# A convolution, state-space, attention and expert kernel: Silu by Tanh on ScalarE, with the multiplications on VectorE one stage later

## The chip, the cores and the metric

The kernel runs on one core of a Trainium2 chip. The core has a matrix engine (TensorE, PE in the profile; its loads of weights are PEld), a vector engine (VectorE, DVE), a scalar engine for activation functions (ScalarE, ACT), a fourth compute engine (GpSimd, POOL) and an engine that here only starts transfers (SyncE, SP). Each engine works through its own instructions in their order and waits on semaphores for the others. The metric is the device time of one execution in microseconds (us); the time before is the median of four runs.

## The reference

The input is x of 4 images with 128 channels and 64 x 64 pixels, in float32. Layer 0 normalises x, runs a depthwise 3 x 3 convolution with a Gelu and a matrix, and then a state-space block ("mamba") over the 4096 pixels of an image in four groups of 32 channels. Layer 1 is attention with four heads over the 4096 pixels, followed by eight experts of which two are chosen for each pixel. The part that the change touches is the input of the state-space block:

```
xz = u @ in_proj_w.T
xin, z = jnp.split(xz, 2, axis=-1)
xin = conv_general_dilated(pad(xin), conv1d_w, ...)      # 4 taps along the pixels
xin = jax.nn.silu(xin + conv1d_b[None, :, None])
x_dbl = xin @ x_proj_w.T
dt, Bm, Cm = jnp.split(x_dbl, [R, R + N], axis=-1)
delta = jax.nn.softplus(dt @ dt_proj_w.T + dt_proj_b)
dA = jnp.exp(delta[..., None] * A)
dBu = delta[..., None] * Bm[:, :, None, :] * xin[..., None]
h = dA_t * h + dBu_t ;  y = einsum("bdn,bn->bd", h, C_t) # scan over the pixels
out = y * jax.nn.silu(z) @ out_proj_w.T                  # y with D_skip * xin added
```

Silu(v) is v times the logistic function of v, which is the same as v/2 + v/2 tanh(v/2).

## The kernel before

The pixels of an image are cut into 8 blocks of 512, so there are 32 blocks for the four images. A block's state-space work is split into two halves (p = 0 and 1) of 128 partitions, and a half has 16 states (n). One block, half and state is a unit; there are 1024 units.

The main loop (line 1207) goes through slots, one unit in each. In a slot the engines get, in this order: a read of `rows` (two rows of the state-space matrices, broadcast to all partitions) for the unit three slots ahead, on SP's queue; the copy of the last state on ACT; the decay `da`, an Exp on ACT, for the unit two slots ahead; one group of attention (four matrix products of scores `sc` on PE and two large Exps `pT` on ACT); the unit's scan on DVE (a product into `h`, a scan over `h`, a product into `hc`); and then, between them, pieces of all other work. An earlier unit's `hc` is summed on PE into `y` (after the first half of the first image POOL adds the `hc` of two units first); the weighted sums `av` of the attention group of the slot before close the PE work.

The other work consists of tasks that are written as generators, in two lanes, X and Y. A lane runs one task at a time, and each `yield` ends one of its pieces. A slot advances each lane by two pieces, in the order X second half, Y first half, [sums of `y`], Y second half, [weighted sums], X first half (lines 1234 to 1251). Every instruction goes through a helper that fixes its place on its engine (lines 428 to 449), so nearly all rows of the profile carry line 445, and the order on each engine is the order in which the Python code emits. Lane Y runs the norms and the convolution of a block (`first_norm`, `conv`) and the input stage of each half (`inputs`, line 679); lane X runs what follows a block (`closed`, line 769: keys, queries and values for attention) and the end of attention with the experts (`finished`, line 1000).

The input stage computes `ps` (two matrix products with `inxc`) and `pz` (one with `inz`) in its first piece; both Silus, into `xin` and `zs`, in its second; the products with `wbc` and `wdt` from `xin` in its third; and in its fourth the copy `bc`, which is sent to memory as `bcd`, and the softplus as Abs, Exp, Ln and Relu (`e`, `ln`, `delta`). One slot later five POOL instructions finish `delta` and `du`. The units of this half can then read `rows` from `bcd`, form `da` from `delta`, and scan with `du`. If a unit's input is not ready when the loop wants to fetch its rows, `until` (line 1149) advances the lanes alone.

PSUM for this work is one bank for each lane (`work("X")` and `work("Y")`); the input stage takes the bank of lane X for `pz` and for the product with `wbc`. The set `held` keeps the lanes out of each other's way: `inputs` and `closed` wait while it isn't empty.

ACT computes its functions from tables. Between a Silu and the next Exp stands a load of another table, and so it is between Exp and Ln, and between Exp and Gelu.

Of the kernel before, what the change touches and what calls it, by code (L numbers as in the profile page):

```python
# [12 lines left out]
AF = mybir.ActivationFunctionType  # L13
ALU = mybir.AluOpType
# [22 lines left out]
def conv_mamba_attn_moe_kernel(ctx: ExitStack, tc: tile.TileContext, t: dict):  # L37
    nc = tc.nc
# [34 lines left out]
    inz, cb, dtb, dsk, wbc = (load(k) for k in ("inz", "cb", "dtb", "dsk", "wbc"))  # L73
# [16 lines left out]
    inxc = const.tile([P, 2, P], F32, name="inxc")  # L90
    for j in range(4):
        r = slice(DI * (j % 2), DI * (j % 2) + DI)
        nc.vector.tensor_mul(inxc[r, j // 2, :], inx[r, :], cw[r, j, :])

    amat = const.tile([P, NST], F32, name="amat")
    nc.scalar.activation(amat, alog, AF.Exp)
# [342 lines left out]
    class Queue:  # L439
# [7 lines left out]
    tensor, vector, scalar, gpsimd, sync = (  # L447
        Queue(e) for e in (nc.tensor, nc.vector, nc.scalar, nc.gpsimd, nc.sync)
    )
# [40 lines left out]
    def tmp(lane, name, shape=None):  # L490
        return side.tile(shape or [P, BLK], F32, tag=f"tmp{lane}", name=name, bufs=4)
# [38 lines left out]
    held = set()  # L530
# [148 lines left out]
    def inputs(b, i, p):  # L679

        xn, pairs = xn_of[b, i], pairs_of[b, i]
        r = slice(DI * p, DI * p + DI)
        while held:
            yield
            yield
        held.add("in")
        ps = work("Y")
        summed(ps, [(inxc[:, j, :], pairs[:, p, 2 * j : 2 * j + BLK]) for j in range(2)])
        pz = work("X")
        mm(pz, inz[r, :], xn[r, 3 : 3 + BLK])  # L690
        yield
        xin = mix.tile([P, BLK], F32, name="xin", bufs=2)
        scalar.activation(xin, ps, AF.Silu, bias=cb)
        zs = mix.tile([P, BLK], F32, name="zs", bufs=4)
        scalar.activation(zs, pz, AF.Silu)
        yield

        pb = work("X")
        mm(pb[0:DI, :], wbc, xin)
        ps = work("Y")  # L700
        mm(ps, wdt, xin)
        yield
        held.clear()
        bc = tmp("Y", "bc")[0:DI, :]
        scalar.copy(bc, pb[0:DI, :])
        bcd = dram.tile([2, NST, 2 * BLK], F32, name="bcd", bufs=4)
        send(bcd.rearrange("c n (k q) -> (c n k) q", k=2), bc)

        e = tmp("Y", "e")
        scalar.activation(e, ps, AF.Abs, bias=dtb)  # L710
        scalar.activation(e, e, AF.Exp, scale=-1.0)
        ln = tmp("Y", "ln")
        scalar.activation(ln, e, AF.Ln, bias=1.0)
        delta = mix.tile([P, BLK], F32, name="delta", bufs=2)
        scalar.activation(delta, ps, AF.Relu, bias=dtb)
        yield
        yield

        du = mix.tile([P, BLK], F32, name="du", bufs=2)
        lost = du  # L720
        gpsimd.tensor_scalar(lost, e, 1.0, -1.0, ALU.add, ALU.add)
        gpsimd.tensor_sub(lost, e, lost)
        gpsimd.tensor_add(ln, ln, lost)
        gpsimd.tensor_add(delta, delta, ln)
        gpsimd.tensor_mul(du, delta, xin)
        in_of[b, i, p] = xin, zs, delta, du, bcd
        done.add(("in", b, i, p))
        yield
# [40 lines left out]
    def closed(b, i):  # L769

        if i == 0:
            kqv[b] = [], [], [], dram.tile([P, NTILE * C], F32, name="td")
        kd, qd, vd, td = kqv[b]
        j, u = divmod(i, 2)
        if u == 0:
            kd.append(dram.tile([P, 2, 2 * BLK], F32, name=f"kd{j}"))
            qd.append(dram.tile([P, 2, 2, 2 * BLK], F32, name=f"qd{j}"))
            vd.append(dram.tile([NH, 2, P, NT * 2 * DH], F32, name=f"vd{j}"))
        kd, qd, vd, sj = kd[j], qd[j], vd[j], slice(u * BLK, (u + 1) * BLK)
        s = slice(i * BLK, (i + 1) * BLK)  # L780
        cm = tmp("X", "cm")
        vector.scalar_tensor_tensor(
            cm.rearrange(IMAGE, w=IMG), xn_of[b, i][:, 3:].rearrange(IMAGE, w=IMG), skip,
            y0_rows(b, i), ALU.mult, ALU.add,
        )
        xr = load_x(t["xtok"][b], i, "xr")
        yield
        yield
        ps = work("X")
        for p in range(2):  # L790
            r = slice(DI * p, DI * p + DI)
            mm(ps[r, :], wout[:, p, r], gated.pop((b, i, p)))
        done.add(("freed", b, i))
        yield
        vector.tensor_add(cm, ps, cm)
        gpsimd.tensor_add(by_tile(xr), by_tile(xr), projb[:, None, :].to_broadcast([P, NT, C]))
        yield
        while held:
            yield
            yield  # L800
        held.add("closed")
        ps = transposed("X", by_tile(cm))
        yield
        xt = yield from normalised("X", by_tile(ps))
        held.clear()
        ps = transposed("X", xt)
        yield
        f = tmp("X", "f")
        scalar.activation(f, ps, AF.Identity, bias=lnb, scale=lnw)
        yield  # L810
        ps = work("X", [P, NT, C])
        for j in range(NT):
            mm(ps[:, j, :], f[:, j * P : (j + 1) * P], projT)
        yield
        tt = side.tile([P, NT, C], F32, name="tt")
        vector.tensor_add(tt, ps, by_tile(xr))
        send(tsave[b][:, s], tt.rearrange("p j c -> p (j c)"), 2)
        xt = yield from normalised("X", tt)

        tr = tmp("X", "tr", [P, NT, C])  # L820
        gpsimd.tensor_add(tr, tt, crow[:, None, :].to_broadcast([P, NT, C]))
        send(td[:, s], tr.rearrange("p j c -> p (j c)"), 2)
        ps = transposed("X", xt)
        yield
        xa = tmp("X", "xa")
        scalar.copy(xa, ps)
        yield
        for d, w, bias in ((kd, wkn, bkn), (qd, wqn, bqn)):
            ps = work("X")
            mm(ps, w, xa)  # L830
            yield
            hi = side.tile([P, BLK], F32R, name="hi", bufs=2)
            vector.tensor_scalar(hi, ps, bias, None, ALU.add)
            lo = side.tile([P, BLK], F32R, name="lo", bufs=2)
            vector.scalar_tensor_tensor(
                lo, ps, bias, hi.bitcast(F32), ALU.add, ALU.subtract
            )
            for half, w in enumerate((hi, lo)):
                w = w.bitcast(F32)
                if len(d.shape) == 4:  # L840
                    send(d[:, :, half, sj], w[:, None, :].to_broadcast([P, 2, BLK]))
                else:
                    send(d[:, half, sj], w)
            yield
        ps = work("X", [P, NT, NH, DH])
        for j in range(NT):
            mm(ps[:, j].rearrange("p h d -> p (h d)"), xa[:, j * P : (j + 1) * P], wv)
        yield
        vector.tensor_copy(vst[:, :, :, 0:DH], ps.rearrange("p j h d -> p h j d"))
        send(vd[:, u].rearrange("h p q -> p h q"), vst.rearrange("p h j d -> p h (j d)"))  # L850
        yield
# [275 lines left out]
    def advance(lane, second):  # L1127

        if inside[lane] != second:
            return False  # L1130
        while True:
            if lane not in running:

                tasks = lanes[lane] if lanes[lane] or slot < len(units) else lanes["X"]
                if not tasks or not all(k in done for k in tasks[0][2]):
                    return False
                key, stages, _ = tasks.popleft()
                running[lane] = key, stages(lane) if callable(stages) else stages
            key, stages = running[lane]
            try:  # L1140
                next(stages)
                inside[lane] = not second
                return True
            except StopIteration:
                assert not second
                done.add(key)
                del running[lane]

    def until(key):
        while key not in done:  # L1150
            flush()
            count = len(done)
            moved = [
                advance(*half) for half in (("X", True), ("Y", False), ("Y", True), ("X", False))
            ]
            assert any(moved) or len(done) > count, key

    blocks = [(b, i) for b in range(B) for i in range(NB)]
# [5 lines left out]
    X, Y = lanes["X"], lanes["Y"]  # L1164
# [42 lines left out]
    while slot < len(units) or due or waiting or left or later or lanes["X"] or running:  # L1207
# [13 lines left out]
        if slot < len(units):  # L1221
# [3 lines left out]
            b, i, p, n = unit  # L1225
# [10 lines left out]
        while due and due[0][0] <= slot:  # L1236
            _, unit, term, first = due.popleft()
            b, i, p, n = unit
# [9 lines left out]
        if waiting:  # L1248
            weighted(waiting)
        waiting = group  # L1250
        advance("X", False)
        while later and later[0][0] <= slot:
            next(later.popleft()[1])
        slot += 1
# [6 lines left out]
    with tc.If(nc.values_load(general[0:1, 0:1]) > 0):  # L1261
# [4 lines left out]
        with tc.For_i(0, B, 1) as b:  # L1266
# [6 lines left out]
            with tc.tile_pool(name="ps_again", bufs=4, space=PSUM) as psum:  # L1273
                for i in range(NB):
                    ps = anew(t_tok[:, NT * i : NT * (i + 1), :], psum)
# [92 lines left out]
```

## Time and profile before

| | |
|---|---|
| median of four runs | 5598.81 us (5596.36 to 5607.02) |
| profiled execution, time | 5593.6 us |
| its span, first to last instruction | 5591.3 us |
| mean granted TensorE clock | 0.945 |
| instructions | 60586 |
| table loads on ACT | 319 in the main part, 409.3 us |
| DVE scan instructions | 1024, 1492 us |
| ACT `pT` | 2048, 1983.7 us |

The page gives the busy time of each engine, the same over 40 equal slices of the span, and groups of equal instructions. A group's row names the line, the engine, the operation, what is written and what is read, the shapes and the count; behind the first bar stand the busy time and the mean duration of one in ns; behind the second the time that the engine was idle just before them, and what ended it. A timeline row has the start, the duration, the instruction and, in brackets, the idle time before it with its releaser. In a view by windows each row is a stretch of time with the busy time of each engine, the granted clock of PE, the share of the transfer engines and GB/s. The chain that ended last covers only the last 12 us here and is not used.

The span falls into a start without attention (to about 390 us), a stretch up to 670 us where attention has begun and pauses, the long middle, and from 4957 us on an end in which the scans are done and attention and the experts finish.

### The profile page before, as it was taken

The page shows a single profiled execution, that of the slowest core. Times are in us where ns is not written, and L with a number is a line of the kernel's source. Part 1 is how long each engine was busy: PE and PEld are TensorE (multiplying, and loading weights), DVE is VectorE, ACT ScalarE, POOL GpSimd, SP SyncE. Part 2 cuts the span into 40 slices and gives each one's busy share as a digit, 9 for nine tenths or more (in the row PEclk, how much of TensorE's full clock was granted, in tenths as well). Part 3 has the DMA queues.
Part 4 walks back from the last instruction along what each step waited for, and adds up shares of the span by engine and source line. Part 5 has one row for each costly group of instructions (what it writes and reads, how often), then busy time and mean ns, then how long its engine had stood idle before and what let it go on. Part 6 is the DMA issues. An engine that isn't in the chain of part 4 may idle for free. (4 is left out here: it accounts for less than half of the span.)

```text
span 5591.3 us, 60586 instructions
## 1 busy us (share of the span) xinstructions
PE 4909.8 (88%) x17866; PEld 2038.1 (36%) x17866; DVE 4177.6 (75%) x6275; ACT 3892.6 (70%) x5957; POOL 2160.5 (39%) x1885
## 2 busy tenths in 40 slices
PE   4666798998999898999998899898999999899997
PEld 2222233333333333333333333333333333344443
DVE  4888877887888888888887888887888888741221
ACT  3455587777777777788777777687777777766553
POOL 2333444454444444445443444345444443320000
PEclk7777799999999999999999999999999999999998
DMA  2455565666666666666665556666666666654432
GB/s 94 168 172 175 193 208 209 208 220 216 230 207 202 216 211 214 209 223 232 224 213 192 196 199 210 219 220 213 230 224 207 204 202 209 211 183 154 148 121 67
DMA packets 427635, 1097.91 MB, mean 196 GB/s; under 512 B 48401, under 2 KB 131746, under 8 KB 427298
## 3 DMA queue, kind: packets, MB, share of 16 engines
q1 hardware_dynamic: 426130, 1093.17, 58.0%
q8 instruction: 144, 2.36, 0.2%
q14 instruction: 193, 1.58, 0.1%
q10 hardware_dynamic: 1168, 0.80, 0.0%
HBM read 941.95 MB, written 135.00 MB: 193 GB/s over the span
## 5 line engine op out<-in xcount | busy, mean ns | idle before, releaser
L445 ACT ACTIVATE pT<-sc 128x1024 f32<-128x1024 f32 x2048 | 1983.7, 1022 | 1011.1 <-PE sc L445 1008.6
L445 PE MATMUL av<-pT,v 128*64 128x512 f32 x8192 | 2001.4, 609 | 3.5 <-ACT avs L445 3.4
L445 DVE TENSOR_TENSOR_SCAN h<-da,state,h 128x512 f32<-128x512 f32 x896 | 1310.3, 1462 | 114.7 <-ACT da L445 22.8
L445 PE MATMUL sc<-qs,ks 128*128 128x512 f32 x4096 | 1304.0, 439 | 98.3 <-DMA ks<-kd 53.6
L445 POOL TENSOR_TENSOR hc<-hc 128x512 f32<-128x512 f32 x448 | 654.8, 1462 | 1722.8 <-DVE hc L445 1516.4
L445 PEld LDWEIGHTS sc<-qs,ks 128*128 128x128 f32 x4096 | 715.8, 193 | 771.2 <-ACT pT L445 282.1
L445 PEld LDWEIGHTS av<-pT,v 128*64 128x64 f32 x8192 | 501.7, 137 | 1194.5 <-issue 1104.0
L445 DVE TENSOR_TENSOR h<-rows,du 128x512 f32<-128x512 f32 x1024 | 834.2, 815 | 87.2 <-ACT state L445 36.9
L445 DVE TENSOR_TENSOR hc<-rows,h 128x512 f32<-128x512 f32 x1024 | 804.1, 785 | 78.2 <-DVE h L445 2.3
L445 ACT ACTIVATE da<-delta,amat 128x512 f32<-128x512 f32 x1024 | 749.4, 732 | 9.5 <-DVE h L445 5.2
L445 PE MATMUL y<-hc,ident 128*128 128x512 f32 x1152 | 665.8, 666 | 62.1 <-DVE hc L445 51.3
L445 ACT ACT_TABLE_LOAD x319 | 409.3, 1283 | 23.2 <-PE ps_Y L445 18.0
L445 ACT COPY state<-h 128x1 f32<-128x1 f32 x896 | 175.6, 196 | 194.6 <-DVE h L445 193.9
L445 PEld LDWEIGHTS y<-hc,ident 128*128 128x128 f32 x1152 | 219.9, 210 | 213.9 <-DVE hc L445 101.7
L445 POOL TENSOR_SCALAR rsY<-mvY 128x4 f32<-128x4 f32 x99 | 57.1, 576 | 523.3 <-DVE mvY L445 519.3
L445 POOL TENSOR_TENSOR avs<-avs,prev 128x512 f32<-128x512 f32 x64 | 91.8, 1434 | 430.3 <-ACT avs L445 306.1
L445 PE MATMUL ps_X<-share,w_ew 128*128 128x512 f32 x448 | 225.4, 626 | 20.5 <-DVE share L445 19.8
L445 ACT ACTIVATE xt<-ps_Y,shiftY,rsY 128x128 f32<-128x128 f32 x380 | 143.3, 462 | 133.0 <-POOL shiftY L445 125.5
L445 POOL TENSOR_SCALAR du<-e 128x512 f32<-128x512 f32 x64 | 146.0, 2282 | 215.2 <-ACT e L445 215.2
L445 DVE TENSOR_TENSOR share<-share,xf 128x1024 f32<-128x1024 f32 x128 | 181.9, 1421 | 52.0 <-DMA share<-sharesY 30.3
L445 DVE RECIPROCAL den<-den 128x32 f32<-128x32 f32 x16 | 5.5, 347 | 265.4 <-DMA den<-total 265.3
L445 DVE TENSOR_TENSOR_SCAN h<-da,h 128x512 f32<-128x512 f32 x128 | 181.7, 1419 | 15.5 <-ACT da L445 2.5
(234 smaller groups left out, 4722.3 us busy)
## 6 DMA issues: line engine op xcount, KB each, us to landing
rows<-bcd SPq DMA_DIRECT2D x1024, 512.0 KB
ks<-kd SPq DMA_DIRECT2D x256, 512.0 KB
qs<-qd SPq DMA_DIRECT2D x129, 512.0 KB
v<-vd SPq DMA_DIRECT2D x256, 256.0 KB
share<-sharesX SPq DMA_DIRECT2D x112, 512.0 KB
pairs<-xn SPq DMA_DIRECT2D x128, 128.5 KB
qd<-hi SPq DMA_DIRECT2D x32, 512.0 KB
qd<-lo SPq DMA_DIRECT2D x32, 512.0 KB
```

Source lines behind the costliest of these rows:

```text
L445: return lambda *args, **kw: queued(op(*args, **kw))
```

## The change

The weights `inxc`, `inz` and the bias `cb` are halved once at the start, so that `ps` with its bias and `pz` hold v/2. ACT computes Tanh of both. Two half slots later DVE computes, with scalar_tensor_tensor, xin = (ps + cb) * t, then xin = (ps + cb) + xin, and zs = (zs + 1) * pz. The stage's later pieces move back by one slot. Since `pz` now stays in lane X's bank for a slot longer, a new member "z" of `held` stops lane X's first half from advancing until DVE has read it. The sets are emptied by name instead of as a whole.

```
+    for w in (inxc.rearrange("p j c -> p (j c)"), inz, cb):
+        nc.vector.tensor_scalar_mul(w, w, 0.5)
...
-        held.add("in")
+        held.update(("in", "z"))
...
         xin = mix.tile([P, BLK], F32, name="xin", bufs=2)
-        scalar.activation(xin, ps, AF.Silu, bias=cb)
+        t = tmp("Y", "t")
+        scalar.activation(t, ps, AF.Tanh, bias=cb)
         zs = mix.tile([P, BLK], F32, name="zs", bufs=4)
-        scalar.activation(zs, pz, AF.Silu)
+        scalar.activation(zs, pz, AF.Tanh)
+        yield
+        yield
+        vector.scalar_tensor_tensor(xin, ps, cb, t, ALU.add, ALU.mult)
+        vector.scalar_tensor_tensor(xin, ps, cb, xin, ALU.add, ALU.add)
+        vector.scalar_tensor_tensor(zs, zs, 1.0, pz, ALU.add, ALU.mult)
+        held.discard("z")
         yield
...
-        held.clear()
+        held.discard("in")
...
-        held.clear()
+        held.discard("closed")
...
-            moved = [
-                advance(*half) for half in (("X", True), ("Y", False), ("Y", True), ("X", False))
-            ]
+            moved = [advance("X", True), advance("Y", False), advance("Y", True)]
+            moved.append("z" not in held and advance("X", False))
...
-        advance("X", False)
+
+        if "z" not in held:
+            advance("X", False)
```

## The prediction

> **What bounds the kernel now.** I read the busy time of the engines first, then the stretches, then the neighbourhood of the instructions that change. The page (engine, busy us, share; then busy tenths in 40 slices of 140 us):
>
> ```profile
> PE 4909.8 (88%) x17866; PEld 2038.1 (36%) x17866; DVE 4177.6 (75%) x6275; ACT 3892.6 (70%) x5957; POOL 2160.5 (39%) x1885
> ...
> PE   4666798998999898999998899898999999899997
> ...
> DVE  4888877887888888888887888887888888741221
> ACT  3455587777777777788777777687777777766553
> ```
>
> TensorE (PE) leads in all but the first five slices; there VectorE (DVE) does. Three stretches (us of each engine in the order PE, PEld, DVE, ACT, POOL, then the granted clock):
>
> ```profile
> 390.00:670.00 280.00, 189.36 (x456) 76.68 (x458) 238.48 (x335) 146.13 (x275) 108.73 (x96) 0.76 0.53 180
> 670.00:4860.00 4190.00, 3809.93 (x14232) 1581.38 (x14230) 3457.38 (x5043) 3171.47 (x4877) 1857.23 (x1569) 0.97 0.63 213
> 4960.00:5420.00 460.00, 447.87 (x1810) 189.14 (x1810) 91.14 (x250) 270.50 (x322) 38.30 (x51) 0.99 0.44 143
> ```
>
> From 670 to 4860 us PE is busy 91%, DVE 83%, ScalarE (ACT) 76%. Ten of the 64 input stages lie before 670 us; I look at the 52 that follow (Silu at 679 to 4674 us) and leave the last two out. The rows that the change touches (count, busy us, mean ns), and two of the operation that it adds:
>
> ```profile
> L445 ACT ACT_TABLE_LOAD x319 | 409.3, 1283 | 23.2 <-PE ps_Y L445 18.0
> ...
> L445 ACT ACTIVATE xin<-ps_Y,w_cb 128x512 f32<-128x512 f32 x64 | 44.0, 688 | 31.6 <-PE ps_Y L445 30.9
> ...
> L445 ACT ACTIVATE zs<-ps_X 128x512 f32<-128x512 f32 x64 | 37.8, 591 | 6.8 <-PE ps_X L445 6.5
> ...
> L445 DVE SCALAR_TENSOR_TENSOR lo<-ps_X,w_bkn,hi 128x512 fp32r<-128x512 f32 x32 | 24.0, 751 | 1.1
> ...
> L445 DVE SCALAR_TENSOR_TENSOR cm<-ps_Y,w_fc2b,y 128x512 f32<-128x512 f32 x32 | 23.8, 742 | 13.8 <-PE ps_Y L445 13.8
> ```
>
> I cut the trace at the start of the Silu of each of the 52 stages and summed 5 us windows: 0 to 5, 5 to 10 and 10 to 15 us after it.
>
> ```profile
> sum 260.00, PE 245.88 PEld 89.76 DVE 186.38 ACT 232.82 POOL 80.96; mean PE 4.73 PEld 1.73 DVE 3.58 ACT 4.48 POOL 1.56
> sum 260.00, PE 255.05 PEld 92.95 DVE 154.22 ACT 236.03 POOL 89.50; mean PE 4.90 PEld 1.79 DVE 2.97 ACT 4.54 POOL 1.72
> sum 260.00, PE 200.47 PEld 75.98 DVE 186.03 ACT 256.70 POOL 239.78; mean PE 3.86 PEld 1.46 DVE 3.58 ACT 4.94 POOL 4.61
> ```
>
> ACT is full (90, 91, 99%), DVE has 4.9 us of 15 free, and PE idles, but mostly in the third window (23%). Whether the table loads cause that idling is the whole question. A typical stage:
>
> ```profile
> 2382.84 1.28 ACT L445 ACT_TABLE_LOAD   x1
> 2384.13 0.69 ACT L445 ACTIVATE xin<-ps_Y,w_cb 128x512 f32<-128x512 f32 x1
> 2384.72 0.59 ACT L445 ACTIVATE zs<-ps_X 128x512 f32<-128x512 f32 x1
> 2385.32 1.28 ACT L445 ACT_TABLE_LOAD   x1
> 2386.62 0.72 ACT L445 ACTIVATE da<-delta,amat 128x512 f32<-128x512 f32 x1
> 2387.69 1.94 ACT L445 ACTIVATE pT<-sc 128x1024 f32<-128x1024 f32 x2 [0.35 <-PE sc L445]
> ...
> 2390.16 0.69 ACT L445 ACTIVATE e<-ps_Y,w_dtb 128x512 f32<-128x512 f32 x1
> ```
>
> ```profile
> 2389.00 1.12 PE L445 MATMUL ps_Y<-xin,wdt 128*128 128x512 f32 x2
> 2397.03 0.73 PE L445 MATMUL sc<-qs,ks 128*128 128x512 f32 x2 [1.18 <-ACT pT L445]
> ```
>
> The two loads around the Silus are absorbed: by `pT` ACT waits for PE again, and `e` starts 0.04 us after the matmul `wdt` ends (2390.12). PE's idle 1.18 us comes from what follows: `e`, Exp, load, Ln, Relu, load, `da`, `pT`, 6.87 us against 5.73 us of PE work. The change leaves that chain as it is. Of the 52 stages 35 show less than 0.11 us from the end of `wdt` to `e`; in the other 17 it is 0.47 to 2.28 us, 17.6 us in all.
>
> **The change part by part, in us.**
>
> *Removed.* Tanh needs no load next to Exp: the built program has 193 table loads, before 320. 127 x 1.283 = 163 off ACT. On the path is only what delays `e`: at least 0, at most both loads in each of the 52 stages, 52 x 2.57 = 134. I take the 17.6 measured, and 7 for the clock: after 7 of those 17 stages the granted clock is 0.5 for 27 in all, half of which is lost, and I give half of that back. -25. *The trace and a rule:* In the rows above `da` starts 0.02 after the load before it has ended. The Trainium skill (ScalarE: Activation LUTs, What ACT_TABLE_LOAD costs) adds a drain of about 1380 ns to every load, 2.66 us a switch; by it 338 would leave ACT, and the upper bound would be 277. No drain shows here, so the sum goes by 1.283.
>
> *Tanh for Silu.* Same shapes and operands, priced like the Silu rows (688 and 591 ns): 0. The loads also waited for PE's matmul; Tanh waits for it itself.
>
> *Added on DVE.* 192 scalar_tensor_tensor at 0.745 (the rows lie at 742 and 751): 143, 2.24 a stage. They stand a slot after the Tanhs, behind that slot's scan. What hides them in the 52 stages is DVE's lead. I measured it as the time from the end of a slot's `hc` to PE's first score two slots on: median 8.7; in the slots from one before the input stage to two after it at least 9.0, median 10 to 14; from three to eight slots after it at least 4.2 (stages from slot 200 on). In before DVE reaches that place between 4.3 before and 4.3 after the Silu's start, about when both Tanhs would end (1.28 of load less, 1.28 of two Tanhs), so that what it may wait there fits into the lead too. Cost 0; without the lead 52 x 2.24 = 116. Behind them in DVE's queue stands the next slot's `h`, for which ACT's copy of the state and PE's sum `y` wait, both after the lead. In the ten stages before 670, where DVE is the bound (85% from 390 to 670), it is 0 to 10 x 2.24 = 22; in the 15 us after the Silu DVE is idle 3.0 a stage there (last 8 of the ten), which hides a part. I take +10.
>
> *Moved.* `wbc`, `wdt`, `bc`, `e` to `du` and the send of `bcd` come one slot later, and following both slot loops I find that the stage of half p = 0 also begins one slot later (the longer stage of p = 1 stands before it in lane Y): two slots in all, three at the first block of an image. What is late next is `da` of that half, which stands in ACT's queue ahead of `pT`. From the end of POOL's `delta` to that `da` before shows 5.2 to 48, median 14. The two slots ahead of that `da` last 7.4 in the median. Of the 27 blocks after 670 us two fall short when 8.1 goes off, 3.7 in all, and thirteen when 14.6 does (three slots of 4.86), 44 in all. I take +5. SP's read of `rows` still comes a slot or more after the send of `bcd`. Lane X loses one slot a stage; it is idle in 299 of 1024 scan slots before and in 247 after: 0.
>
> *Order of attention.* Before, attention finds its keys unready in slots 465 to 469; on resuming PE waits 5.9 for `ks`, and two stretches of 6.8 at half clock (6.8 lost) lie there. In the changed loop those empty slots don't occur (1200 slots instead of 1204, attention starting one later). Bounds 0 and -13; I take -12, since the work itself only moves.
>
> *Setup.* Three small multiplies, and two DVE steps (1.5) in the first chain against one load saved (1.28): 0.
>
> Sum: -25 + 10 + 5 - 12 = -22. The profiled execution took 5593.6 (span 5591.3), 5.2 under the median of 5598.81; so 5571.6 for it and 5577 for a median.
>
> **Rivals.**
> 1. *All loads count* (gain 134 instead of 25). For it: ACT at 90% and more for 15 us, DVE idle beside it. Against: PE at 95 and 98% in the first 10 us, `e` on time in 35 of 52. 5598.8 - 134 - 12 + 15 = 5468; with half of it, 5535.
> 2. *No change.* PE bounds these stages, and what ACT gains is waited away at the same `pT`; the empty slots come back elsewhere. For it: the same idle 1.18 us after the Ln chain. Against: the 17 late stages. 5599.
> 3. *Slower: `delta` is late.* With input stages 14.6 later ACT stands at `da`, `pT` behind it and PE behind that: 44, and after each of the 13 waits half clock for 3.4, 13 x 1.7 = 22; with DVE's part before 670 in full (22) and the 25 + 12 gained kept: +51, 5650. With a shift of 12.5 ten blocks fall short by 20 in all: 20 + 17 + 22 - 37 = +22, 5621. It decides from a shift of about 10 (2 short blocks at 9.7, 10 at 12.5). Against: ACT waited for `delta` once so far, 2.3 us.
> That the loads stay is ruled out by the program.
>
> **How the numbers follow.** Forecast 0.48, rival 1 0.12, rival 2 0.17, rival 3 0.23. The predicted time is the forecast's, 5577; its own range is 5560 to 5592. The range to hold 8 in 10 reaches past half of rival 1 and the lower form of rival 3: 5525 to 5625. Within 0.2% is 5587.6 to 5610.0, about what a measurement can tell from no change; an edge of the forecast (0.03) lies in it. Faster 0.45 + 0.12 = 0.57, same 0.20, slower 0.23.
>
> **What would show it.** 193 loads and some 247 us in their row; ACT 160 less busy, DVE some 140 more; `e` within 0.1 us of `wdt` in nearly all stages; PE's idle of about 1.2 us before `sc` still there; DVE's lead never under 2 us; no large wait of ACT `da` for POOL `delta`. Wrong is the forecast if PE's idle time from 670 to 4860 us (380 us now) falls by much more than 30 us, if ACT waits for `delta` in more than a few blocks, or if PE waits for `xin` behind DVE.

## The result, and the profile after

The changed kernel takes 5603.64 us (median of 39 runs, 5589.63 to 5622.63); the kernel before, measured beside it, 5596.43 us (60 runs). The ratio is 1.0014, with a 95% interval of 1.0009 to 1.0019: slower by 7.8 us, where 22 us less were forecast. The profiled execution has a span of 5601.4 us (5591.3 before) at a mean granted clock of 0.946 (0.945).

The busy times on the page of the changed kernel, with PE, DVE and ACT in the 40 slices (here 140 us each):

```profile
PE 4903.2 (88%) x17866; PEld 2057.2 (37%) x17866; DVE 4332.8 (77%) x6470; ACT 3735.2 (67%) x5830; POOL 2166.8 (39%) x1885
...
PE   4666698998899899998999899898989899999997
...
DVE  4889887888888888888898888888888888851221
ACT  2444577777777677677677667677667777766553
```

ACT has lost 157 us of work and DVE has gained 155. PE's busy time fell by 6.6, but the span grew by 10.1. The same two stretches as before:

```profile
390.00:670.00 280.00, 179.59 (x433) 73.17 (x431) 243.95 (x342) 130.95 (x260) 104.66 (x90) 0.79 0.53 181
670.00:4860.00 4190.00, 3810.04 (x14254) 1602.34 (x14256) 3588.42 (x5188) 3040.12 (x4768) 1857.19 (x1568) 0.97 0.63 213
```

In the long middle PE is busy 3810.0 us, as before (3809.9): what ACT gave up there did not let PE run more. In the stretch up to 670 us DVE is busier by 5.5 us and PE by 9.8 less. The changed rows of the page's groups, ACT first:

```profile
L448 ACT ACTIVATE pT<-sc 128x1024 f32<-128x1024 f32 x2048 | 1983.9, 1022 | 1117.2 <-PE sc L448 1114.4
...
L448 ACT ACT_TABLE_LOAD x192 | 246.3, 1283 | 3.4
...
L448 ACT ACTIVATE t<-ps_Y,w_cb 128x512 f32<-128x512 f32 x64 | 43.9, 686 | 56.3 <-PE ps_Y L448 55.9
L448 ACT ACTIVATE zs<-ps_X 128x512 f32<-128x512 f32 x64 | 38.1, 596 | 25.8 <-PE ps_X L448 25.8
```

```profile
L448 DVE SCALAR_TENSOR_TENSOR xin<-ps_Y,w_cb,xin 128x512 f32<-128x512 f32 x64 | 48.1, 751 | 2.3
L448 DVE SCALAR_TENSOR_TENSOR xin<-ps_Y,w_cb,t 128x512 f32<-128x512 f32 x64 | 47.8, 747 | 39.6 <-ACT t L448 39.4
...
L448 DVE SCALAR_TENSOR_TENSOR zs<-zs,ps_X 128x512 f32<-128x512 f32 x64 | 43.4, 678 | 1.1 <-ACT zs L448 1.1
```

192 loads are left of 319, and the new operations cost what the rows before had promised: 139 us on DVE, 82 on ACT. The first row says where the 163 us of loads went. Before, it read:

```profile
L445 ACT ACTIVATE pT<-sc 128x1024 f32<-128x1024 f32 x2048 | 1983.7, 1022 | 1011.1 <-PE sc L445 1008.6
```

ACT's idle time ahead of `pT`, always until PE delivers `sc`, rose by 106 us: two thirds of the freed time is now waiting for PE. A stage of the changed kernel, ACT alone:

```profile
2407.67 0.69 ACT L448 ACTIVATE t<-ps_Y,w_cb 128x512 f32<-128x512 f32 x1 [0.18 <-PE ps_Y L448]
2408.73 0.60 ACT L448 ACTIVATE zs<-ps_X 128x512 f32<-128x512 f32 x1 [0.37 <-PE ps_X L448]
2409.22 0.71 ACT L448 ACTIVATE da<-delta,amat 128x512 f32<-128x512 f32 x1
2412.37 1.94 ACT L448 ACTIVATE pT<-sc 128x1024 f32<-128x1024 f32 x2 [2.44 <-PE sc L448]
...
2420.83 1.28 ACT L448 ACT_TABLE_LOAD   x1
```

No load stands around the Tanhs any more, and ACT waits 2.44 us for PE behind them and one `da`.

How far the two executions are at the same unit shows where the difference arises. The columns are the starts of four scans and the end of the last `pT`, in us; a slot is counted by the unit that is scanned in it, 256 to an image:

| | slot 150 | 256 | 512 | 1023 | last `pT` |
|---|---|---|---|---|---|
| before | 673.6 | 1145.1 | 2413.6 | 4956.3 | 5516.1 |
| after | 678.5 | 1153.6 | 2436.7 | 4981.1 | 5527.5 |

8.5 us are lost in the first image (up to slot 256), 14.6 from there to 512, next to nothing (1.7) from 512 to the last scan, and 13.4 come back in the tail. The tail and the middle belong together: attention has no empty slots at 465 to 469 any more, so that 252 `pT` lie between slots 384 and 512 instead of 240, and 303 instead of 312 are left for the tail.

### The profile page after: what moved, and what is told of

The parts are those of the page before. It is cut to its first block, busy times and chain, and to the rows that moved or that the text cites. A ratio compares the mean times of both kernels' runs of the same rounds, so it can differ in the third digit from the quotient of the medians.

```text
span 5601.4 us, 60582 instructions
## 1 busy us (share of the span) xinstructions
PE 4903.2 (88%) x17866; PEld 2057.2 (37%) x17866; DVE 4332.8 (77%) x6470; ACT 3735.2 (67%) x5830; POOL 2166.8 (39%) x1885
## 4 chain that ended last, share of the span: by engine, by line
PE 46%; DVE 24%; ACT 11%; issue 7%; POOL 6%; DMA 5%; SPq 1%; DVEq 0%; ACTq 0%; POOLq 0%
PE av L448 17%; DVE h L448 12%; PE sc L448 10%; PE ps_X L448 9%; PE ps_Y L448 5%; PE y L448 4%; ACT pT L448 3%; ACT xt L448 2%; DVE hc L448 2%; DVE cm L448 2%; ACT L448 2%; POOL rsX L448 2%; POOL rsY L448 1%; DMA inv<-inverse 1%; ACT e L448 1%
## 5 line engine op out<-in xcount | busy, mean ns | idle before, releaser
L448 PE MATMUL sc<-qs,ks 128*128 128x512 f32 x4096 | 1312.2, 441 | 65.1 <-ACT pT L448 35.5
L448 DVE TENSOR_TENSOR_SCAN h<-da,state,h 128x512 f32<-128x512 f32 x896 | 1291.8, 1442 | 97.1 <-ACT da L448 6.5
L448 DVE TENSOR_TENSOR h<-rows,du 128x512 f32<-128x512 f32 x1024 | 867.2, 847 | 38.5 <-DMA rows<-bcd 14.9
L448 PE MATMUL y<-hc,ident 128*128 128x512 f32 x1152 | 644.7, 646 | 61.1 <-DVE hc L448 55.5
L448 POOL TENSOR_SCALAR rsY<-mvY 128x4 f32<-128x4 f32 x99 | 56.8, 573 | 658.4 <-DVE mvY L448 656.1
L448 PE MATMUL ps_X<-ident,xt 128*128 128x128 f32 x372 | 95.5, 329 | 120.3 <-ACT xt L448 113.2
```

What stands on the lines that cost most here:

```text
L448: return lambda *args, **kw: queued(op(*args, **kw))
```

## The experiments

All ratios are to the kernel before, measured beside it on the same chip; in brackets is the 95% interval. Behind a ratio, us are the ratio less 1, times 5596. Each run has one profile, of one execution; its span can lie some us off the run's median. Two suspects stood at the start: the new order (a longer stage, lane X held) and DVE's added work; open was whether the table loads had been worth anything.

**New order alone.** The changed kernel, but ACT computes Silu as before, without halved weights and without the multiplications.

```
-        t = tmp("Y", "t")
-        scalar.activation(t, ps, AF.Tanh, bias=cb)
+        scalar.activation(xin, ps, AF.Silu, bias=cb)
...
-        scalar.activation(zs, pz, AF.Tanh)
+        scalar.activation(zs, pz, AF.Silu)
...
-        vector.scalar_tensor_tensor(xin, ps, cb, t, ALU.add, ALU.mult)
-        vector.scalar_tensor_tensor(xin, ps, cb, xin, ALU.add, ALU.add)
-        vector.scalar_tensor_tensor(zs, zs, 1.0, pz, ALU.add, ALU.mult)
```

> The new order alone: the input stage is one slot longer and lane X is held back with z as in the changed kernel, but ACT computes Silu as before (320 table loads) and DVE gets no multiplications. Theory A (the loads were worth the 25 us predicted, and the longer stage with lane X held costs about 36): ratio to before 1.004 (+24 us = 36 - 12 for the empty attention slots). Theory B (loads worth nothing, the multiplications on DVE cost what was lost): 0.998 (-12 us). Theory C (loads worth nothing, the order costs about 10): 1.000, and lane X's waits (PE ps_X for DVE prX, for ACT xt and xf) as long as in the changed kernel.

Measured 1.0003 [0.9994, 1.0012], +1.7 us. The size is theory C's, but the next run speaks against its other half, that the loads are worth nothing. The scan of slot 150 starts at 658.4, 15 us earlier than before: the longer stage helps the first image (it does so alone too, further down). And though all 319 loads are there, `e` starts within 0.04 us of the end of `wdt` in every stage from 670 us on but the last. What cured the late `e` is the new order, not the missing loads.

**Loads back.** The changed kernel with a Silu of one column ahead of the Tanhs.

```
+        scalar.activation(spare, spare, AF.Silu)
         scalar.activation(t, ps, AF.Tanh, bias=cb)
```

> The changed kernel with a Silu of one column ahead of the two Tanhs in each input stage, so that the two table loads per stage are back (about 320 loads, 1.28 us each, 163 us of ACT), and the rest as in the changed kernel. Theory A: +18 to +25 us on the changed kernel, ratio to before 1.005 to 1.006, and e comes late again in some stages. Theory B and C: within 6 us of the changed kernel, ratio 1.001 to 1.0025. If all loads count: +134 us, ratio 1.025.

Measured 1.0045 [1.0031, 1.0059], 17 us above the changed kernel, a little under theory A. But no `e` is late here either, again but for the last. The page of this run:

```profile
PE 4913.0 (87%) x17866; PEld 2055.0 (37%) x17866; DVE 4328.0 (77%) x6470; ACT 3904.9 (70%) x6021; POOL 2169.6 (39%) x1886
```

Its span is 5616.5, 15.1 above the changed kernel's, and 9.8 of that is PE's busy time for the same 17866 matmuls. Stretches at half clock between 670 and 4860 us sum to 242 us here and to 222 in the changed kernel. Each of the 55 stretches here follows 3.4 us in which PE was busy 61% or less (91% is the mean from 670 to 4860 us). So in these two profiles the loads cost less by waiting than by the lower clock that PE is granted after waiting. A second pair further down, Silu in the first image without and with the loads behind it, agrees: 14.8 of the 24.0 us between its spans are PE's busy time. How much of this is the chance of single executions is open: the kernel before, with all its loads, has the same 242 us.

**DVE's work twice.** The changed kernel with three more multiplications a stage.

```
+        junk = side.tile([P, BLK], F32, name="junk")
+        vector.scalar_tensor_tensor(junk, ps, cb, t, ALU.add, ALU.mult)
+        vector.scalar_tensor_tensor(junk, ps, cb, t, ALU.add, ALU.add)
+        vector.scalar_tensor_tensor(junk, t, 1.0, pz, ALU.add, ALU.mult)
```

> The changed kernel with three more multiplications of the same shapes on DVE in each input stage, into a tile that nobody reads (192 more, 2.24 us a stage, 143 us of DVE). Theory A and C (DVE's work is hidden by its lead behind 670 us and costs only in the first image, 8.5 us measured for the first three): +8 to +12 us on the changed kernel, ratio to before 1.003. Theory B (DVE's work is what costs): +20 us or more, ratio from 1.005 up, to 1.024 if none of it is hidden.

Measured 1.0134 [1.0118, 1.0151], 67 us above the changed kernel for 140 us of DVE. This is far from hidden: in the two profiles 20 us arise before slot 150, 28 before 256, 46 before 512. Not all of it is the price of DVE's time: the new multiplications also read the lanes' two banks, and PE waits 14.9 us for `junk` itself before it can write lane X's.

**Lane X not held.** ACT copies `pz` out of lane X's bank.

```
-        held.update(("in", "z"))
+        held.add("in")
...
+        zc = mix.tile([P, BLK], F32, name="zc", bufs=1)
+        scalar.copy(zc, pz)
...
-        vector.scalar_tensor_tensor(zs, zs, 1.0, pz, ALU.add, ALU.mult)
-        held.discard("z")
+        vector.scalar_tensor_tensor(zs, zs, 1.0, zc, ALU.add, ALU.mult)
```

> The changed kernel in which ACT copies pz out of lane X's bank right behind its Tanh (64 copies more, about 0.6 us each by the zs row, 38 us of ACT) and DVE multiplies from the copy, so that z is no longer held and lane X loses no slot. Theory A (holding lane X is what costs): ratio to before 0.995 to 0.999, the waits of PE ps_X for DVE prX back to about 25 us. Theory B: no gain, 1.001 to 1.004. Theory C: 0.999 to 1.000 if it is the hold, 1.001 or more if it is the longer stage.

Measured 1.0042 [1.0028, 1.0056], 16 us above the changed kernel. Freeing lane X did not help; with 37 us of copies on ACT in the same run it is not shown what the hold alone costs. PE's waits for `prX` fell from 47.0 only to 36.9.

**Silu in the first image.** (`cbf` is a copy of the bias, made before the halving.)

```
+        if b == 0:
+            scalar.activation(xin, ps, AF.Silu, bias=cbf, scale=2.0)
+            scalar.activation(zs, pz, AF.Silu, scale=2.0)
+        else:
+            scalar.activation(t, ps, AF.Tanh, bias=cb)
+            scalar.activation(zs, pz, AF.Tanh)
...
+        if b > 0:
             vector.scalar_tensor_tensor(xin, ps, cb, t, ALU.add, ALU.mult)
...
```

> The changed kernel, but for the first image (16 of the 64 input stages, all before slot 256) ACT computes Silu of twice the halved input, so that DVE gets no multiplications there; the other three images and the order of all work are as in the changed kernel. If the multiplications cost their time only where DVE is the bound, in the first image (19 to 24 us by the two looks that differ in them alone), and the loads there cost nothing: 19 to 24 us below the changed kernel, ratio to before 0.997 to 0.998, faster than both. If the multiplications cost evenly over the stages (16 of 64): about 6 us below the changed kernel, ratio 1.000. If the loads are worth as much in the first image as elsewhere: 4 us less gain than the first.

Measured 0.9997 [0.9986, 1.0008]: 9.5 us below the changed kernel, level with before. In its profile slot 150 is reached 15 us earlier (663.5), slot 256 also 15. The ratio gives less than the 19 to 24 expected for a price paid in the first image alone, and its uncertainty of some 7 us reaches to the 6 us of a price spread evenly over the stages.

**Longer stage alone.** The kernel before with two empty pieces.

```
         scalar.activation(zs, pz, AF.Silu)
+        yield
+        yield
```

> The kernel before with its input stage one slot longer (two empty pieces behind the Silus), without the hold on lane X, and nothing else changed (320 loads, no multiplications on DVE). If it is the longer stage that lets the first image end 15 us earlier and brings attention past its empty slots: scan of slot 150 at about 658 us as with the new order alone, ratio to before 0.999 to 1.001. If the hold on lane X cost something on top: up to 10 us below the new order alone, ratio 0.9985. If delta came late by the shift: over 1.003, with waits of ACT da for POOL delta beyond 10 us.

Measured 0.9992 [0.9981, 1.0002], -4.5 us, the low end. Slot 150 starts at 650.7, 23 us earlier than before. Most of it is given back: the stretch from slot 150 to 256 takes 6 more, the tail 10 more (318 `pT` left instead of 312). Of the 54 stages behind 670 us 8 still have an `e` more than 0.11 us behind `wdt`, 8.9 us in all (19 and 20.2 us before, the last two stages with them): the longer stage alone cures only a part.

**DVE's work alone.** The kernel before with three more multiplications in each stage.

```
         mm(ps, wdt, xin)
         yield
+        junk = side.tile([P, BLK], F32, name="junk")
+        for _ in range(3):
+            vector.scalar_tensor_tensor(junk, xin, cb, xin, ALU.add, ALU.mult)
```

> The kernel before with three scalar_tensor_tensor of 128x512 more on DVE in each input stage, into a tile that nobody reads (xin as input, no PSUM), everything else as before. If the first image pays for them in full and the rest hides them: +19 to +24 us, ratio 1.0034 to 1.0043, nearly all of it before slot 256. By the prediction's value (a third of them hidden in the first image as well, 0 behind it): +10 us, 1.0018. If nothing is hidden: +143 us, 1.026.

Measured 1.0055 [1.0039, 1.0071], +31 us. In the profile 10 of it have arisen by slot 150, 15 by slot 256, and the rest behind the first image, where the prediction had put 0. (These multiplications are dearer than the change's own, 872 ns; see the last section.)

**Stage as short as before.** The changed kernel without the two slot halves.

```
         scalar.activation(zs, pz, AF.Tanh)
         yield
-        yield
         vector.scalar_tensor_tensor(xin, ps, cb, t, ALU.add, ALU.mult)
...
         mm(ps, wdt, xin)
-        yield
         held.discard("in")
```

> The changed kernel with the two slot halves taken out again: the multiplications come one half earlier, and the products with wbc and wdt in the same half as the softplus chain, so that the stage is as long as before; z still holds lane X for a slot. If the longer stage costs something in the changed kernel (delta late, attention moved): 5 to 10 us below it, ratio to before 0.9995 to 1.0005. If the longer stage gains 15 us in the first image, as the new order alone showed: 5 to 15 us above the changed kernel, 1.002 to 1.004. If ACT now waits for the products (e directly behind wdt in its queue): more than that, with a wait of ACT e for PE ps_Y of 1 us a stage or more.

Measured 1.0088 [1.0075, 1.0101], 41 us above the changed kernel. Slot 150 starts at 705.6, 27 us later. ACT's idle time ahead of `e` is 26.7 in all (24.2 in the changed kernel), so the third case is out; the first image loses. The stage's added slot is a gain, and without it the changed kernel is 41 us slower.

**DVE's work behind the first image, in one burst or spread.** The kernel before with 144 multiplications more.

```
+    flat = taps.rearrange("p k c -> p (k c)")[:, 0:BLK]
+    def burn():
+        junk = side.tile([P, BLK], F32, name="junk")
+        for _ in range(3):
+            vector.scalar_tensor_tensor(junk, flat, cb, flat, ALU.add, ALU.mult)
...
         mm(ps, wdt, xin)
         yield
+        if b > 0:
+            burn()
```

The spread kernel has one multiplication in `burn` and calls it in the main loop:

```
         advance("Y", True)
+        if 256 <= slot < 1024 and slot % 16 in (0, 5, 10):
+            burn()
```

> The kernel before with three scalar_tensor_tensor of 128x512 more on DVE in each of the 48 input stages of the last three images (144 in all, into a tile that nobody reads, inputs in SBUF), none in the first image. The prediction's step (DVE's lead hides them): within 4 us of before, ratio 1.000. If they delay the pieces of lane X and Y that PE waits for on DVE: +12 to +20 us, ratio 1.002 to 1.0036, with PE's waits of ps_X for DVE and ACT pieces some 10 us longer and the scan of slot 150 where before has it (674 us).

> The same 144 scalar_tensor_tensor more on DVE in the last three images, but one at a time in every fifth slot or so (slots 0, 5 and 10 of each 16) instead of three in a row in the slot of the input stage. If the sum of DVE's work counts: as the three in a row, +12 to +20 us. If the burst of 2.24 us is what delays lane X and a single 0.75 us fits between: less than half of the three in a row, 0 to +8 us, ratio below 1.0015.

In a burst 1.0036 [1.0023, 1.0049], +20 us; spread 1.0072 [1.0059, 1.0085], +40. The lead doesn't hide this work, and spreading it, which I expected to be cheaper, costs twice as much. That fits the prediction's finding that DVE has more time beside the input stage than elsewhere; but the spread multiplications also stand at another place in the slot, and what of the difference is due to that isn't shown. In the spread run's profile PE idles 403 us from 670 to 4860 us (380 before), and its busy time for all matmuls is 17 us more, with 290 us at half clock there (242 before). The order of all instructions on PE, ACT and POOL is that of the kernel before, so PE's waits from 670 to 4860 us can be set side by side (engine, what waits, for what: us in total, times, longest). Before:

```profile
PE ps_X L445 <- ACT xt L445: 51.2, 43, 4.0
...
PE ps_X L445 <- DVE prX L445: 23.1, 13, 9.0
...
PE ps_X L445 <- DVE share L445: 19.8, 16, 2.4
...
PE ps_X L445 <- DVE aT L445: 12.7, 6, 5.2
```

With the burst:

```profile
PE ps_X L445 <- ACT xt L445: 56.5, 44, 4.0
...
PE ps_X L445 <- DVE prX L445: 30.5, 16, 10.1
PE ps_X L445 <- DVE share L445: 24.9, 21, 2.4
...
PE ps_X L445 <- DVE aT L445: 18.1, 6, 7.0
```

These four, all for products into lane X's bank, grow by 23.2 us; `xt` itself is made by ACT from statistics that come from DVE through POOL. PE's whole idle time in this stretch grows from 380 to 393, since other waits shrink (the one for `ks` from 41.1 to 35.3). The scan, on the other hand, keeps its lead: from the end of `hc` to PE's first score two slots on it is 8.7 us in the median before, 8.6 with the burst, 8.8 in the changed kernel and 8.6 with DVE's work twice.

**Longer stage in the first image only,** by one slot and by two.

```
         scalar.activation(zs, pz, AF.Silu)
+        if b == 0:
+            for _ in range(4):
+                yield
```

(these lines are the second kernel's; the first has two empty pieces)

> The kernel before with its input stage one slot longer in the first image only (two empty pieces behind the Silus where b is 0), nothing else changed. If the longer stage is what let the first image end 15 to 23 us earlier in the two looks that have it: scan of slot 150 at 650 to 660 us, and 12 to 20 us below before, ratio 0.9965 to 0.998, faster than both kernels. If that gain is given back between slots 150 and 512: ratio 0.999 to 1.000.

> The same with two slots more instead of one in the first image. If what helps is only that DVE's queue gets past the wait for the input chain: no further gain, within 5 us of one slot more. If delta and du come late for the next half: 5 us or more slower than one slot more, with waits of DVE h for POOL du and of ACT da for POOL delta before 670 us.

One slot: 0.9998 [0.9987, 1.0008]; slot 150 at 658.1, but the gain is gone by the end. Two slots: 0.9983 [0.9974, 0.9992], 9.5 us below before, and the only kernel here whose interval lies below 1. Its slot 150 starts at 651.5, the last `pT` ends at 5502.6, and from 104 us to the end of the first image neither DVE nor ACT waits for a late `du` or `delta`. Why two slots keep their gain and one doesn't, these runs don't show.

**The loads back behind the first image.** The run with Silu in the first image, plus

```
         else:
+            scalar.activation(spare, spare, AF.Silu)
             scalar.activation(t, ps, AF.Tanh, bias=cb)
```

> The changed kernel with Silu on ACT in the first image (as in the earlier run of that kind), and in the other three images a Silu of one column ahead of the Tanhs, so that all 320 table loads are back. Against the run without these loads it gives the loads' worth behind the first image: 15 to 17 us if they add up (ratio to before 1.0025 to 1.003). Against the new order alone (1.0003) it gives what the multiplications cost behind the first image: +13 us if they add up, 0 if DVE's lead hides them (ratio 1.0003).

Measured 1.0021 [1.0011, 1.0030]. Without these loads it was 0.9997: they are worth 13 us. Against the new order alone (1.0003) the multiplications behind the first image cost 10 us; the two intervals together leave some 7 us either way. Both near what was expected if the terms add.

This pair has the change's own order and its own multiplications, and PE works through the same instructions in the same order in both. From slot 256 to slot 1023 PE idles 340 us with the new order alone and 355 here. With the new order alone, from 670 to 4860 us:

```profile
PE ps_X L446 <- ACT xt L446: 62.5, 43, 3.6
PE ps_X L446 <- DVE prX L446: 48.3, 17, 5.0
...
PE ps_X L446 <- DVE cm L446: 17.5, 14, 2.2
```

With the multiplications behind the first image:

```profile
PE ps_X L450 <- ACT xt L450: 68.5, 43, 3.8
PE ps_X L450 <- DVE prX L450: 48.7, 17, 5.4
...
PE ps_X L450 <- DVE cm L450: 20.8, 18, 2.6
```

Here it is `xt` and `cm` that PE waits for longer; `prX`, `share` (22.6 to 20.7) and `aT` (16.9 to 16.6), which grew with the burst, don't. The wait for `prX`, 23.1 before, has doubled by the new order alone.

**The hold alone.** The kernel before with `z` held from the first piece of the stage to the third.

```
-        held.add("in")
+        held.update(("in", "z"))
...
         scalar.activation(zs, pz, AF.Silu)
         yield
+        held.discard("z")
...
-        advance("X", False)
+        if "z" not in held:
+            advance("X", False)
```

> The kernel before with the hold z on lane X alone: set with the input stage's first piece, released in its third, so that lane X loses one slot a stage; stage length, Silu, loads and DVE's work as before. If lane X's lost slot costs what the difference of two runs says: +6 us, ratio 1.001. If the prediction's 0 holds: 1.000 within 0.0005. If it moves attention as the new order does (no empty slots at 465 to 469): tail after the last scan about 547 us instead of 560.

Measured 1.0005 [0.9995, 1.0015], +3 us with 0 inside the interval: as a price of the hold inconclusive. What it does to attention is plain: 303 `pT` are left after the last scan, in 548 us. So it is the hold, not the longer stage (318 left), that brings attention past its empty slots, and this run is the test of that term: -12 was predicted for it, with 0 for the hold, and the interval from -3 to +8 leaves that out. The hold alone also makes `e` late more often, in 34 of the 54 stages.

**Both.** Silu, no hold and two slots more in the first image, the changed stage in the others.

```
         if b == 0:
             scalar.activation(xin, ps, AF.Silu, bias=cbf, scale=2.0)
             scalar.activation(zs, pz, AF.Silu, scale=2.0)
...
+        if b == 0:
+            held.discard("z")
+            yield
+            yield
```

> First image: Silu on ACT, no hold on lane X, the input stage two slots longer (the run with that alone was at 0.9983). Other images: as in the changed kernel, with Tanh and the multiplications on DVE. If the terms add: 0.9983 plus what the changed stage is worth behind the first image (-17 loads, +13 multiplications, +5 hold, all of it within 5 us of 0): ratio 0.9975 to 0.9990, faster than both kernels. If attention's order eats it: 0.9995 or more.

Measured 0.9995 [0.9985, 1.0006]. This is what was expected if the gain of the longer first image is not kept; the interval still reaches into the range of terms that add. Of the kernels measured the one to use is the one before with two slots more in the first image.

## Why the prediction was wrong

Four runs lie on a path from before to after, each step changing one main thing:

| step | predicted, us | measured, us |
|---|---|---|
| before to the new order alone: `delta` later (+5), empty slots (-12), lane X held (0) | -7 | +1.7 |
| to the multiplications in images 2 to 4 (loads still there) | 0 | +10 |
| to the multiplications in the first image too | +10 | +13 |
| to the kernel without the loads | -25 | -17 |
| sum | -22 | +7.8 |

The second and third steps also hold Tanh for Silu and the small Silus that bring the loads back (203 ns each on ACT); the fourth takes these out again. Each step is a difference of two ratios with some 5 to 10 us of uncertainty; the sum is the measured result. By that the first two steps lie clear of their forecast, by 8.7 us with an uncertainty of 5 and by 10 with 7; the last two don't.

- **The step that failed** is "What hides them in the 52 stages is DVE's lead ... Cost 0". The lead was measured for one product of DVE, the scan's `hc`, and there the reasoning was right: it stays at 8.6 to 8.8 us. But DVE also makes what lane X and lane Y pass on to PE (`prX`, `share`, `aT`, `cm`, statistics for `xt`), and for these PE does wait. In the place of 0 the runs show +10 us (3 to 17) in the change's own order, where PE's idle time behind the first image grows by 15 us, at `xt` and `cm` among others, and +20 for the burst in the order of before, where four of these waits grow by 23 us. How much lead each of these products has was not measured.
- **A second term failed: the empty slots.** -12 was forecast. The waits that I counted went (PE for `ks` from 41.1 to 13.4 us), but the groups of attention that fill these slots cost as much as they did in the tail or more: 22 to 34 us more between slots 384 and 512 in the profiles with the hold, against 10 to 13 off the tail. I had counted the waits that go and left out the groups that come. The hold alone, which has this term, measured +3 (-3 to +8).
- **Loads removed** had its sign right; the size is -17 (-26 to -9) for -25, and 13 (5 to 22) for the loads behind the first image. Its ground was wrong. The 17 late stages vanish with the new order, loads or not, and where lane X isn't held 8 late ones stay, 8.9 us with the loads (longer stage alone) and 8.8 without them (lane X not held). In the profiles most of what the loads still cost is PE's busy time at a lower clock (9.8 of 15.1 us between two spans, 14.8 of 24.0 in the other pair).
- **The first image** was well placed: +10 predicted within 0 to 22, 13 and 9.5 measured by two differences, each with 7 to 9 us of uncertainty.
- **The order otherwise.** `delta` late: ACT's `da` waits for it 8.8 us in six places, 2.3 in one before, so at most +6.5 where +5 was said. Lane X's lost slots were put at 0; PE's wait for `prX` doubled with the new order (23.1 to 48.3 us), and that for `xt` into lane X's bank went from 51.2 to 62.5. It isn't the hold alone (11.8 for `prX`, but 82.4 for `xt`) nor the longer stage alone (31.3 and 60.7). And the longer stage gained 15 to 23 us in the first image, which no step had; alone it was worth 4.5 in the end.
- Right were: the number and price of the loads, ACT -157 (160 said), `e` within 0.1 us of `wdt` in all stages but one (0.14) and the last. PE's idle ahead of `sc` that ends with `pT` is still there, 35.5 us in all, but was 44.4 before. PE's idle from 670 to 4860 us stayed at 380 as the sum of opposite moves: less for `ks` and `pT`, more for `prX` and `xt`. DVE's +155 is 16 over the multiplications: `h` got dearer, 847 ns for 815 (33 us), the scan cheaper by 20 us. The new order alone does this to `h` (847 ns) and has 55 us more of DVE than before without an added instruction, which no term of the prediction had. The lead, said never to fall under 2 us, does so in two slots (in three before).

The rival of late `delta` had the sign, but not the cause: its wait is 8.8 us in all, not 44. The rival of no change came nearest, at 5599 us, and both of its reasons show: two thirds of what ACT gained is waited away at `pT`, and the empty slots came back elsewhere. But the loads were worth something, and it came near because DVE's work, for which it had no term, took that back.

## What to carry to other kernels

A lead that is measured for one product of an engine hides only work ahead of that product: list everything that the engine hands to the bottleneck, and price added work at the product with the least slack. Time freed on an engine that already waits for the bottleneck mostly becomes more waiting (106 of 163 us here), so price a removal by what it does to the bottleneck's idle time and clock. When an edit also shifts the order of a hand-scheduled loop, run the shift alone: here the changed kernel without its added slot was 41 us slower, more than any part of the exchange itself, and a shift in one image alone gave the best kernel.

## What the hardware showed

DVE multiplications of the same size take nearly the same time in the median (746 and 752 ns below), and differ beside a POOL addition by where their operands lie. The change's own, with one operand in PSUM, by minimum, median and maximum:

```profile
L448 DVE SCALAR_TENSOR_TENSOR xin<-ps_Y,w_cb,t x64: 739/746/753, 85.0 to 4857.5; 128x512 f32<-128x512 f32 x64
```

The burst's, with both in SBUF:

```profile
L445 DVE SCALAR_TENSOR_TENSOR junk<-taps,w_cb x144: 717/752/1840, 1113.9 to 4862.3; 128x512 f32<-128x512 f32 x144
```

24 of the 144 take more than 1.2 us, and beside each of them POOL is in an addition of two tensors (`hc`, `xr` or `tr`) that began less than a us earlier (once 0.03 us later); the DVE instruction ends 0.55 us after that one. Over the 144 the mean is 910 ns for a median of 752, 23 us in all, so the runs with such multiplications overstate the change's DVE time by about a fifth. `h`, with both operands in SBUF, varies in the same way (626 to 1789 ns before): 132 of its 1024 take more than 1.2 us before and 166 after, each ending 0.55 us after a POOL addition. So its mean moves with the order. Of the change's second multiplications (`xin` from `ps_Y` and `xin`, one of them in PSUM) 29 ran beside a POOL addition of `hc` and took 751 ns in the mean, as without one. The Trainium skill (GPSIMD Engine Reference, Specifications) says that POOL shares its SBUF interfaces with VectorE, with contention for instructions that have two SBUF inputs. The rows above agree.
